# Mixing two batches' expert weights from one load, a deeper second layer for the third batch, and two-operand sums on GpSimd in an attention and feed-forward kernel

## The chip, the cores and the metric

The kernel runs on one core of one Trainium2 chip, in 32-bit floating point. The metric is the device time of one execution in microseconds (us). The kernel before the change took 3223.96 us, the median of 3 runs (3223.83 to 3225.29).

A core has five engines that run their own instruction queues in order and wait for each other by semaphores: TensorE (PE in the profile, its weight load PEld), VectorE (DVE), ScalarE (ACT), GpSimd (POOL) and SyncE (SP), which in this kernel issues all DMA transfers.

## What is computed

Four batches of 2048 tokens with 512 features go through two residual sub-layers:

```python
x = x + layernorm(attention(layernorm(x), w_qkv))   # 16 heads, windows of 128, keys of 3 windows
x = x + layernorm(ffn(layernorm(x), ...))

def ffn(x):                                   # 512 -> 2048 -> 512, 8 experts' weights mixed per batch
    g = (relu(x @ gate_w1.T + gate_b1) @ gate_w2.T + gate_b2).mean(axis=1)     # 8 numbers per batch
    mW1 = W1 + einsum('be,efh->bfh', g, TW1);  mb1 = b1 + g @ Tb1
    mW2 = W2 + einsum('be,ehf->bhf', g, TW2);  mb2 = b2 + g @ Tb2
    return gelu(x @ mW1.T + mb1) @ mW2.T + mb2
```

So each batch has weights of its own: the base plus eight experts' weights, each times one gate number. The gate numbers are means over the whole batch, so a batch's weights can be mixed only when its attention and its gate are through.

## The kernel before

**Attention stage** (the first half). It walks 256 *slots*: 64 windows of 128 tokens, four groups of four heads each. A slot puts the scores of the next slot (`scores`, L649, then the row maximum `nm`, L658, on VectorE), the transposes of this slot's probabilities (L686), some "dense" products (the projections of a later block of 512 tokens, or the gate's, L518), the exponentials (L671) and the values (L707) in a written order. What else a slot does hangs in lists by slot number: `first`, `mid`, `aux`, `rest`, `behind`, `late`; the program runs them in the order `first`, scores, transposes, `mid`, exponentials, `aux`, dense products, `rest`, the read of the second bank, weight mixing, the read of the first bank, `behind`, values, `late`.

The dense products use a Winograd form (seven half-size products for eight), which needs four sums of the transposed tokens for each block: T1 and T2 (`right_factors` part 0, L482 and L483) and T3 and T4 (part 1, L486 and L487). Both parts come once for the projections and once for the gate of a block, that is twice in 16 slots.

Each window's attention output is normalized and added to its input in `residual` (L103, L330), stored to memory, and its statistics are taken for the next normalization (`stats`: L92 and L94 on VectorE, then two one-column operations on GpSimd, L96 and L98). `normed` overwrites the same tile one slot later, so it waits for the store.

**Weight mixing** is a generator, `blend = mixer()`, that other code advances by `next(blend)`. Its order is batch, layer (`s`), chunk of 2 x 128 rows (`c`, 8 of them), expert (`e`, 8). A *step* is either one expert (one 512 KB load, issued three steps ahead into four buffers named `exps`, and one `scalar_tensor_tensor` of 128x1024 on VectorE, L155) or, after the eighth expert, the four sums that the Winograd form of the weights needs (L163 to L166, 128x256 each); the stores of a chunk are issued with the next step. In the attention, slots from 85 on take steps by the list `MIXED` (21 steps in 16 slots).

**Feed-forward stage** (the second half). It walks 16 blocks K of 512 tokens, four per batch. Each has a first layer (four sets of seven 256-wide products, L1023, in `begin`, `middle`, `end`, with the mixing steps put between products) and a second layer. For batches 0 to 2 the second layer is `second`: seven products (L1143), each 32 matmuls of 256 columns in the trace. For the last batch (`DEEP`) it is `second_deep`: Winograd applied twice, so 7 x 7 products of 128 columns (L1308), with more sums: `inner_sums` (L1233) on VectorE for the tokens' side, four GpSimd sums into `t1` at outer product `o == 2` (L1344), and `inner_mixer` (L205 to L208) for the weights' side, 14 steps that load, sum and store again what `mixer` stored. `more_sums` (L1105, L1106, L1111) and `second` (L1181, L1187) put two-operand sums on GpSimd.

Of the kernel before, what the change touches and what calls it, by code (L numbers as in the profile page):

```python
# [16 lines left out]
P = 128  # L17
# [17 lines left out]
def sandwich(ctx: ExitStack, tc: tile.TileContext, x, w_qkv, gw1, gb1, gw2, gb2, w1, b1, w2, b2, tw1, tb1, tw2, tb2, out):  # L35
# [23 lines left out]
    gw1_sb = const.tile([P, KC, D], F32, name="gw1_sb")  # L59
# [20 lines left out]
    DEEP = (NB - 1,)  # L80
# [24 lines left out]

    def mixer():

        todo = [(b, s, c, e) for b in range(NB) for s in range(2) for c in range(HC) for e in range(NX)]
        ets, accs = {}, {}
# [5 lines left out]
        def load(n):  # L115
            b, s, c, e = todo[n]
            base, exps = ((w1, tw1), (w2, tw2))[s]
            if e == 0:
                acc = mix.tile([P, 2, D], F32, tag="acc", name=f"acc_{b}_{s}_{c}")
                nc.sync.dma_start(acc, halves(base)[c])  # L120
                accs[b, s, c] = acc
            et = mix.tile([P, 2, D], F32, tag="exps", bufs=4, name=f"exps_{b}_{s}_{c}_{e}")
            nc.sync.dma_start(et, halves(exps[e])[c])
            ets[n] = et
# [20 lines left out]
        for n in range(3):  # L145
            load(n)
        yield
        for n, (b, s, c, e) in enumerate(todo):
            if n + 3 < len(todo):
                load(n + 3)  # L150
            for f in late:
                f()
            late = []
            acc = accs[b, s, c]
            nc.vector.scalar_tensor_tensor(acc, ets.pop(n), g_all[b][:, e : e + 1], acc, ALU.mult, ALU.add)  # L155
            yield
            if e == NX - 1:
                del accs[b, s, c]
# [4 lines left out]
                nc.vector.tensor_tensor(sums[:, 0, :], a21, a22, ALU.add)  # L163
                nc.vector.tensor_tensor(a21, a11, a21, ALU.subtract)
                nc.vector.tensor_tensor(sums[:, 1, :], sums[:, 0, :], a11, ALU.subtract)
                nc.vector.tensor_tensor(sums[:, 2, :], a12, sums[:, 1, :], ALU.subtract)  # L166
                late.append(lambda b=b, s=s, c=c, acc=acc, sums=sums: store(b, s, c, acc, sums))
                yield
        for f in late:
            f()  # L170

    issued = {b: 0 for b in DEEP}

    def inner_mixer(b):

        todo = [(o, h) for o in order_deep for h in range(2)]
        loaded, late = {}, []

        def load(n):
            o, h = todo[n]  # L180
            two = slice(2 * h, 2 * h + 2)
            et = mix.tile([P, 4, 2, P], F32, tag="exps", bufs=4, name=f"inner_{b}_{o}_{h}")
            nc.sync.dma_start(et[:, :2], m3_d[b][:, o, 0:8:7, two, :])
            nc.sync.dma_start(et[:, 2:], m3_d[b][:, o, 3:7:3, two, :])
            loaded[n] = et

        def store(n, et):
            o, h = todo[n]
            two = slice(2 * h, 2 * h + 2)
            nc.sync.dma_start(m3_d[b][:, o, 1, two, :], et[:, 3])  # L190
            nc.sync.dma_start(m3_d[b][:, o, 2, two, :], et[:, 0])
            nc.sync.dma_start(m3_d[b][:, o, 4:6, two, :], et[:, 1:3])
            issued[b] = n + 1

        for n in range(2):
            load(n)
        yield
        for n in range(len(todo)):
            for f in late:
                f()  # L200
            if n + 2 < len(todo):
                load(n + 2)
            et = loaded.pop(n)
            f11, f21, f12, f22 = (et[:, i] for i in range(4))
            nc.vector.tensor_tensor(f22, f21, f22, ALU.add)  # L205
            nc.vector.tensor_tensor(f21, f11, f21, ALU.subtract)
            nc.vector.tensor_tensor(f11, f22, f11, ALU.subtract)
            nc.vector.tensor_tensor(f12, f12, f11, ALU.subtract)  # L208
            late = [lambda n=n, et=et: store(n, et)]
            yield  # L210
        for f in late:
            f()

    def gate_matmuls(pm, xT, oc, kcs=range(KC)):
        for kc in kcs:
            nc.tensor.matmul(pm, lhsT=gw1_sb[:, kc, ts(oc, P)], rhs=xT[:, kc, :], start=(kc == 0), stop=(kc == KC - 1))
# [19 lines left out]
    def gate_half(pm, xT, ocs, kcs):  # L236

        for n, oc in enumerate(ocs):
            for kc in kcs[n]:
                nc.tensor.matmul(  # L240
                    pm[:, n * Q : (n + 1) * Q],
                    lhsT=gw1_sb[:, kc, ts(oc, P)],
                    rhs=xT[:, kc, :],
                    start=(n == kc == 0),
                    stop=True,
                    skip_group_check=True,
                )
# [13 lines left out]
    def gate_end(b, hsum, bank, spare):  # L261
# [24 lines left out]

        def first_biases():
# [38 lines left out]
    def residual(W_):  # L326
# [3 lines left out]
        nc.vector.tensor_tensor(x1, x1, st["x"], ALU.add)  # L330
        nc.sync.dma_start(x1_d[W_], x1)
        st["sc"] = stats(x1, f"c{W_}")
# [62 lines left out]
    with ExitStack() as actx:  # L395
# [25 lines left out]
        def load_rest():  # L421
            nc.sync.dma_start(gw1_sb, gw1.rearrange("(k p) o -> p k o", p=P))
# [36 lines left out]
        def left_factors(i):  # L459
            w = wqkv[i] if i < 3 else gw1_sb  # L460
            l11, l12, l21, l22 = (w[:, 2 * j : 2 * j + 2, h * Q : (h + 1) * Q] for h in range(2) for j in range(2))
# [12 lines left out]
        def right_factors(K, part, i=0):  # L474
# [1130 lines left out]
```

## Time and profile before

| what | value |
|---|---|
| median of 3 runs | 3223.96 us |
| the profiled execution | 3224.83 us |
| its span, first to last instruction | 3223.0 us |
| granted TensorE clock | 0.998 of full speed |
| bytes moved by DMA | 688.88 MB, mean 214 GB/s |
| mixing loads (`exps`) | 512 of 512 KB, 6.0 us to landing |

A line of "busy time" gives an engine's busy microseconds, its share of the span and its instruction count. A window line gives, for a stretch, each engine's busy time (with the number of instructions), the granted clock, the DMA engines' share and the rate. The chain of waits is followed back from the last instruction to whatever released it; its lines are start, duration and what ran. A group line gives an operation's count, its busy time and mean duration, and after the second bar the idle time before it and what ended it. A timeline line gives start, duration and the instructions.

### The profile page before, as it was taken

How to read it: one execution, taken by the hardware profiler on the slowest of the kernel's cores; microseconds unless marked ns; L12 is line 12 of the kernel's file. 1: busy time of each engine (PE TensorE's matmuls, PEld its weight loads, DVE VectorE, ACT ScalarE, POOL GpSimd, SP SyncE). 2: the span in 40 equal slices, each digit the busy share in tenths (PEclk: the TensorE clock that was granted, in tenths of full speed). 3: DMA queues.
4: the chain of work that ended last, by engine and by line, in shares of the span. 5: the costliest groups of instructions: out<-in, count | busy, mean ns of one | idle time of the engine just before them, and what ended most of it. 6: DMA issues, size and time to landing. Idle time of an engine off the chain costs nothing.

```text
span 3223.0 us, 61653 instructions
## 1 busy us (share of the span) xinstructions
PE 3197.1 (99%) x23862; PEld 2697.0 (84%) x23862; DVE 2278.8 (71%) x3307; ACT 1576.5 (49%) x4332; POOL 676.5 (21%) x847
## 2 busy tenths in 40 slices
PE   9999999999999999999999999999999999999998
PEld 7788888888788888878768888888888888889998
DVE  5766666888998889888865665677657667554555
ACT  3777777777777777777761222112222112222222
POOL 0111111111111111110112322323322323332233
PEclk9999999999999999999999999999999999999999
DMA  2111112455555556554677889999899999874555
GB/s 87 54 57 54 40 60 80 138 189 163 193 193 168 178 177 200 194 174 151 211 277 277 310 309 345 355 337 330 311 330 361 341 326 322 305 246 155 193 187 170
DMA packets 363334, 688.88 MB, mean 214 GB/s; under 512 B 27161, under 2 KB 115353, under 8 KB 357026
## 3 DMA queue, kind: packets, MB, share of 16 engines
q1 hardware_dynamic: 363042, 684.94, 61.4%
q8 instruction: 189, 3.10, 0.4%
q14 instruction: 103, 0.84, 0.1%
HBM read 567.39 MB, written 117.44 MB: 212 GB/s over the span
## 4 chain that ended last, share of the span: by engine, by line
PE 94%; DVE 2%; DMA 2%; ACT 1%; POOL 0%; issue 0%; SPq 0%; POOLq 0%; DVEq 0%; ACTq 0%
PE pm L518 23%; PE px L1023 13%; PE ptp L686 11%; PE px L1143 7%; PE sc L649 7%; PE pz L1023 6%; PE po L707 5%; PE pz L1143 5%; PE py L1023 3%; PE py L1143 3%; PE px L1308 2%; PE py2b L1143 2%; PE pz L1308 1%; PE pm L582 1%; PE ptx L340 1%; PE pto L311 1%
## 5 line engine op out<-in xcount | busy, mean ns | idle before, releaser
L155 DVE SCALAR_TENSOR_TENSOR acc<-exps,g,acc 128x1024 f32<-128x1024 f32 x512 | 697.1, 1362 | 66.1 <-DMA exps<-in_tw 60.1
L658 DVE TENSOR_REDUCE nm<-sc 128x2 f32<-128x768 f32 (+1 forms) x512 | 449.2, 918 | 206.8 <-PE sc L649 201.8
L671 ACT ACTIVATE pr<-sc,nm 128x384 f32<-128x384 f32 (+1 forms) x1024 | 572.8, 592 | 11.3 <-DVE nm L658 11.1
L691 ACT COPY prT<-ptp 128x512 f32<-128x512 f32 x732 | 382.9, 595 | 281.3 <-PE ptp L686 281.1
L686 PEld LDWEIGHTS ptp<-ident,pr 128*128 128x128 f32 x2944 | 318.0, 141 | 102.3 <-issue 89.8
L686 PE MATMUL ptp<-ident,pr 128*128 128x128 f32 x2944 | 378.7, 278 | 0.0
L1060 ACT COPY py<-px 128x512 f32<-128x512 f32 x63 | 36.0, 571 | 662.6 <-PE px L1023 662.4
L1023 PE MATMUL px<-tT,w 128*128 128x256 f32 x1512 | 350.1, 379 | 0.6 <-DVE cpv L1083 0.6
L1023 PEld LDWEIGHTS px<-tT,w 128*128 128x128 f32 x1512 | 286.9, 190 | 40.0 <-DVE cpv L1083 1.0
L649 PE MATMUL sc<-k,q 32*128 32x384 f32 (+2 forms) x2816 | 243.2, 423 | 3.7 <-ACT pr L671 3.5
L671 ACT ACTIVATION_READ_ACCUMULATOR pr<-sc,nm 128x1 f32 x1024 | 236.5, 231 | 0.0
L1080 DVE TENSOR_TENSOR cpb<-pz,cpb 128x512 f32<-128x512 f32 x63 | 43.4, 689 | 268.8 <-PE pz L1023 240.1
L96 POOL TENSOR_SCALAR ve_b<-mv_b 128x1 f32<-128x1 f32 x64 | 42.8, 669 | 819.2 <-DVE mv_b L94 819.2
L707 PEld LDWEIGHTS po<-prT,v 128*32 128x32 f32 x5888 | 152.2, 110 | 50.9 <-ACT pr L671 25.4
L707 PE MATMUL po<-prT,v 128*32 128x128 f32 x5888 | 189.7, 275 | 0.2
L649 PEld LDWEIGHTS sc<-k,q 32*128 32x128 f32 x2816 | 118.7, 184 | 74.4 <-issue 53.9
L1143 PE MATMUL px<-w2s,u 128*128 128x256 f32 x784 | 175.1, 379 | 0.0
L518 PE MATMUL pm<-xnT,wqkv 128*128 128x256 f32 x720 | 172.2, 382 | 0.0
L1105 POOL TENSOR_TENSOR t<-u 128x512 f32<-128x512 f32 x60 | 79.9, 1332 | 434.8 <-ACT u L1035 434.8
L1143 PEld LDWEIGHTS px<-w2s,u 128*128 128x128 f32 x784 | 149.0, 190 | 20.2
L518 PEld LDWEIGHTS pm<-xnT,wqkv 128*128 128x128 f32 x720 | 132.0, 190 | 16.7
L1074 ACT COPY cpb<-px 128x512 f32<-128x512 f32 x63 | 36.9, 585 | 182.0 <-PE px L1023 182.0
(295 smaller groups left out, 5911.6 us busy)
## 6 DMA issues: line engine op xcount, KB each, us to landing
exps<-in_tw SPq DMA_DIRECT2D x512, 512.0 KB, 6.0
w2s<-m2d SPq DMA_DIRECT2D x168, 512.0 KB, 8.1
w2s<-m3d SPq DMA_DIRECT2D x84, 512.0 KB, 4.7
acc<-in_w SPq DMA_DIRECT2D x64, 512.0 KB, 6.1
x<-in_x SPq DMA_DIRECT2D x64, 256.0 KB, 4.2
m1d<-acc SPq DMA_DIRECT2D x64, 256.0 KB, 6.3
w<-m1d SPq DMA_DIRECT2D x16, 1024.0 KB, 7.9
fxT<-xTd SPq DMA_DIRECT2D x16, 1024.0 KB, 8.5
```

What stands on the lines that cost most here:

```text
L155: nc.vector.scalar_tensor_tensor(acc, ets.pop(n), g_all[b][:, e : e + 1], acc, ALU.mult, ALU.add)
L518: nc.tensor.matmul(bank[u not in chain][:, half, :], lhsT=a[:, kc, ts(half, P)], rhs=b[:, kc, :], start=(u not in (2, 3, 4) and half == kc ...
L649: nc.tensor.matmul(scs[r // 2][:, r % 2, col : col + nj * W], lhsT=q[rows, g, ts(W_ % WB, W)], rhs=k_of[kb][rows, g, j0 * W : (j0 + nj) * ...
L658: nc.vector.tensor_reduce(st["nm"][:, h : h + 2], scs[u][:, :, : nk * W], AX.X, ALU.max, negate=True)
L671: nc.scalar.activation(pr[:, : nk * W], scs[r // 2][:, r % 2, : nk * W], AF.Exp, bias=st["nm"][:, h : h + 1], accum_out=st["den"][:, h : h ...
L686: nc.tensor.transpose(pt[:, r, :], st["pr"][g * 4 + r][:, ts(j, W)], ident)
L691: nc.scalar.copy(prT, pt)
L707: nc.tensor.matmul(po[r * E : (r + 1) * E, n, :], lhsT=v_of[kb][:, jj, h * E : (h + 1) * E], rhs=prT[:, r, :], start=(j == 0), stop=(j == ...
L1023: nc.tensor.matmul(bank[:, f, :], lhsT=factor[:, f, kc * P : (kc + 1) * P], rhs=right[:, kc, :], start=(start and f == 0 and kc == 0), sto ...
L1105: nc.gpsimd.tensor_tensor(t1s[c], b12, us[c][:, :, :Q], ALU.subtract)
L1143: nc.tensor.matmul(bank[:, t, :], lhsT=right(c - c % 2)[:, c % 2, ts(t, P)], rhs=w[:, c % (HC // 2), :], start=(start and c == 0 and t == ...
L1308: nc.tensor.matmul(bank, lhsT=right(p), rhs=w[:, p, :], start=(start and p == 0), stop=True, skip_group_check=True,)
```

## The change

1. **Two batches from one load.** `todo` is written out. Batches 0 and 1 stay as they are. Then come four chunks of batch 2's first layer, all eight chunks of the second layer for batches 2 and 3 together (each expert loaded once, two `scalar_tensor_tensor`), the other four chunks of the first layer for both, and batch 3's first four chunks. Batch 3's sums come two experts into the next chunk. Batch 3's accumulators lie in the gate's weight tile, which is split in two (`gw1_0`, `gw1_1`) and free once the gate is over. A step is now one `scalar_tensor_tensor`; all mixing is over in the first layer of block 8 (before: block 11).
2. **The third batch's second layer is deep too**: `DEEP = (NB - 2, NB - 1)`. Its 14 inner steps run inside `mixer`; those of the last batch run in the first layer of block 9 (before: blocks 11 and 12).
3. **Two-operand sums on GpSimd in the attention**: the residual's add, the T sums of all blocks but the first, and the mixing's four sums (33 chunks of the 64), which there no longer count as a step. The residual's store and statistics move from `rest` to `late` of the same slot.
4. **Step counts**: `MIXED` has 25 steps in 16 slots; in the feed-forward stage a block takes 39 (batch 0) or 37 (batch 1) for 34, a batch's last block 35 for 25, the first 23 for 21.
5. **Inside `second_deep`**: the four sums into `t1` go in twos to `o == 3` and `o == 4`; at `o == 6` the statistics of `y[1]` come after inner product 4 and its add, not before.

The core of the diff:

```diff
-    DEEP = (NB - 1,)
+    DEEP = (NB - 2, NB - 1)
...
+        def chunk(batches, k, c, between=()):
+            waiting = [x for x in todo if x[0] == "later"]
+            for e in range(NX):
+                todo.append(("mix", batches, k, c, e))
+                if e == 1 and waiting:
+                    todo.remove(waiting[0])
+                    todo.append(("sum", *waiting[0][1:]))
+            todo.append(("sum", batches[0], k, c))
+            for b in batches[1:]:
+                todo.append(("later", b, k, c))
+            todo.extend(("inner", *x) for x in between)
+
+        again = [(2, o, h) for o in order_deep for h in range(2)]
+        for b in range(2):
+            for k in range(2):
+                for c in range(HC):
+                    chunk((b,), k, c)
+        for c in range(4):
+            chunk((2,), 0, c)
+        for c in range(HC):
+            chunk((2, 3), 1, c)
+        for c in range(4, HC):
+            chunk((2, 3), 0, c, again[2 * c - 8 : 2 * c - 6])
+        for c in range(4):
+            chunk((3,), 0, c, again[2 * c + 8 : 2 * c + 10])
...
+            elif kind == "mix":
+                batches, s, c, e = what
+                load()
+                et = ets.pop(0)
+                for b in batches:
+                    flush()
+                    assert b in gated
+                    acc = accs[b, s, c]
+                    nc.vector.scalar_tensor_tensor(acc, et, g_all[b][:, e : e + 1], acc, ALU.mult, ALU.add)
+                    yield
...
+                engine = nc.gpsimd if attending[0] else nc.vector
+                engine.tensor_tensor(sums[:, 0, :], a21, a22, ALU.add)
+                engine.tensor_tensor(a21, a11, a21, ALU.subtract)
+                engine.tensor_tensor(sums[:, 1, :], sums[:, 0, :], a11, ALU.subtract)
+                engine.tensor_tensor(sums[:, 2, :], a12, sums[:, 1, :], ALU.subtract)
...
-    def residual(W_):
+    def residual(W_, engine=nc.gpsimd):
         st = win[W_]
         x1 = st["x1"]
         normalize(x1, st["a"], st["sb"])
-        nc.vector.tensor_tensor(x1, x1, st["x"], ALU.add)
-        nc.sync.dma_start(x1_d[W_], x1)
-        st["sc"] = stats(x1, f"c{W_}")
+        engine.tensor_tensor(x1, x1, st["x"], ALU.add)
+
+    def residual_stats(W_):
+        st = win[W_]
+        nc.sync.dma_start(x1_d[W_], st["x1"])
+        st["sc"] = stats(st["x1"], f"c{W_}")
...
-        def right_factors(K, part, i=0):
+        def right_factors(K, part, i=0, engine=nc.gpsimd):
...
-                nc.vector.tensor_tensor(t[:, 0], r12, r11, ALU.subtract)
-                nc.vector.tensor_tensor(t[:, 1], r22, t[:, 0], ALU.subtract)
+                engine.tensor_tensor(t[:, 0], r12, r11, ALU.subtract)
+                engine.tensor_tensor(t[:, 1], r22, t[:, 0], ALU.subtract)
...
+            late[i + 1].append(lambda W_=W_: residual_stats(W_))
...
-        MIXED = (1, 0, 1, 1, 2, 1, 1, 2, 2, 1, 1, 1, 2, 1, 2, 2)
+        MIXED = (2, 1, 1, 2, 2, 1, 1, 2, 2, 1, 1, 2, 2, 2, 1, 2)
...
-                if o == 2:
-                    for p in range(PAIRS2):
+                if o in (3, 4):
+                    for p in range(2 * o - 6, 2 * o - 4):
                         nc.gpsimd.tensor_tensor(t1[:, p], bottom[:, p, :, :Q], t2[p // 2][:, p % 2], ALU.subtract)
...
-                    step = mixing(0, 1, 0, 1)
+                    step = mixing(0, 1, 0, 1) if K == 0 else mixing(1, 1, 1, 1)
                 else:
-                    step = mixing(*((2, 1, 1, 1) if c == 2 else (1, 1, 1, 1)))
-                if K // NBLK in DEEP and k == 0:
+                    step = mixing(*((2, 1, 1, 1) if b == 0 or c > 2 else (1, 1, 1, 1)))
+                if K == DEEP[0] * NBLK + 1:
+                    if c == 0:
+                        assert next(blend, 0) == 0
+                        inner = inner_mixer(NB - 1)
                     step = lambda: next(inner, None)
...
-                products2 = second(K, before, mixing(3, 2, 3, 2, 2, 3, 2), load_x1)
+                products2 = second(K, before, mixing(3, 3, 3, 2, 3, 3, 2), load_x1)
```

## The prediction, made before the changed kernel ran

> **What bounds the kernel.** First the busy times, to see which engine leaves no room:
>
> ```profile
> PE 3197.1 (99%) x23862; PEld 2697.0 (84%) x23862; DVE 2278.8 (71%) x3307; ACT 1576.5 (49%) x4332; POOL 676.5 (21%) x847
> ```
>
> TensorE idles 26 us in 3223, so an edit can gain only by taking TensorE work away, and can lose by making TensorE wait. Then the windows, to see how near the other engines are to full in each stage (attention, batch 1's feed-forward, batch 3's):
>
> ```profile
> core 0: us, PE busy (x) PEld busy (x) DVE busy (x) ACT busy (x) POOL busy (x), PEclk, DMA share, GB/s
> 860.00:960.00 100.00, 100.00 (x961) 80.94 (x961) 90.10 (x132) 73.93 (x219) 13.54 (x24) 1.00 0.59 198
> ...
> 2212.00:2309.00 97.00, 97.00 (x451) 85.41 (x450) 68.56 (x78) 22.55 (x48) 29.24 (x28) 1.00 0.92 332
> ...
> 2980.00:3075.00 95.00, 93.80 (x624) 87.47 (x623) 46.94 (x99) 25.91 (x63) 29.02 (x30) 1.00 0.49 169
> ```
>
> In the attention TensorE is full and VectorE at 90%; it is the engine to overload. In batch 1 VectorE has 28 us of 97 free. The DMA is at 92%, yet TensorE is full: its transfers are hidden. Third, the chain of waits, whose second-layer entries give the length of a block:
>
> ```profile
> 2402.01 5.18 PE px L1143 x24
> ...
> 2499.21 5.18 PE px L1143 x24
> ...
> 2595.90 5.18 PE px L1143 x24
> ...
> 2693.02 5.18 PE px L1143 x24
> ...
> 2789.71 5.18 PE px L1143 x24
> ...
> 2986.57 7.45 DMA fxT<-xTd
> 3080.58 7.16 DMA fxT<-xTd
> ```
>
> Batch 2's blocks are 97.20, 96.69, 97.12 and 96.69 us apart, batch 3's deep ones 94.01. Last, how VectorE and GpSimd get on when both run two-operand operations. VectorE's timeline in block 5, and under it GpSimd's:
>
> ```profile
> 2221.35 2.25 DVE L155 SCALAR_TENSOR_TENSOR acc<-exps,g,acc 128x1024 f32<-128x1024 f32 x1
> 2223.64 1.37 DVE L163 TENSOR_TENSOR sums<-acc 128x256 f32<-128x256 f32 x1
> 2225.05 1.37 DVE L164 TENSOR_TENSOR acc<-acc 128x256 f32<-128x256 f32 x1
> ```
>
> ```profile
> 2222.58 4.96 POOL L1187 TENSOR_TENSOR u<-u,t 128x512 f32<-128x512 f32 x3
> ```
>
> A mixing operation that takes 1.278 us (L155's median) takes 2.25 here, and sums of 0.420 (L163's median) take 1.37: each waits out about 0.95 us of GpSimd's 1.27.
>
> **Part by part.** Sums are against the profiled execution, 3224.8 us (span 3223.0 and 1.8 around it); the median of the runs is 0.9 below it.
>
> *Batch 2 deep (2).* Four blocks of 387.7 us become four like batch 3's: the first 95.1 (its second layer was 1.1 us longer than the next, waiting at its start for the first inner sums), three at 94.0, together 377.1. **-10.6 us.** The inner sums' VectorE work lies where mixing was: block 8 keeps 18 steps, blocks 9 to 11 have none. Bounds: -12 (no such start) and -8 (L1308 waits twice as long).
>
> *Order in `second_deep` (5).* Batch 3 shows TensorE waiting there:
>
> ```profile
> PE px L1308 <- DVE y L1270: 5.7, 9, 1.0
> ```
>
> In TensorE's timeline these stand in each block near 19.6 us into the second layer (0.98, 0.98, 0.98 and 0.5 us), where the four `t1` sums on GpSimd push VectorE back (an inner sum of 0.68 takes 1.47 there), and at `o == 6` behind the statistics (0.55 each, 1.1 in the last). The change moves the sums to two products with two each, and the statistics back. At most -1.5 us in a block; I take -0.9 for the two new collisions, over eight blocks **-7**, bounds -12 and 0. The last block's end is VectorE's, so nothing for it there.
>
> *Sums on GpSimd in the attention (3, 4).* The T sums of the gate come 14 times from 222.7 to 1554.9 us, so 16 slots last 102.5 us. Over 660 to 1460 us VectorE is busy 89.1 of 100 us, thus 91.3 in 16 slots. Removed from it: 4 residual adds x 0.693, 8 T sums x 0.68, 2.33 chunks x 1.69 (21 steps are 2.33 x 9): 12.1. Added: 25 instead of 18.7 mixing operations x 1.278: 8.1. Leaves 87.3, **15.2 us free**. GpSimd gets 12 operations of 128x512 (1.27 us, L1105's median) and 12.5 of 128x256, which no row has: between 0.22 (L96, one column) and 1.27, I take half-way, 0.74. Together 24.5 us in 16 slots, on 13.5. What it costs VectorE by collisions: in the feed-forward stage, with GpSimd busy 29 of 97 us, the mean of L155 is 1.362 over all 512 against a median of 1.278, 43 us on some 312 operations there, 0.14 each; in the attention that makes 25 x 0.14 = 3.5 us. Here GpSimd's sums are issued just ahead of mixing operations, so I double it: 7 us, under 15.2. If every GpSimd operation met one, it would be 12 x 0.95 + 12.5 x 0.6 = 19. TensorE bears some lateness: VectorE's row maximum ends about 1 us before ScalarE uses it, and the exponentials lie ahead of the transposes by 2 us or more. T sums: near 1173 us `rs_b` ends at 1182.35, T3 on GpSimd would then be there by 1183.6, TensorE reads it at 1186.46; 2.8 us of cover, gone where four chunk sums (3 us) or a late VectorE come between. I charge **+3 us** for such stalls in 32 T3 reads, bounds 0 and +20.
>
> The Trainium skill, "SBUF — State Buffer", section "SBUF: two separate sides", speaks against this part: a VectorE operation with two SBUF inputs and a GpSimd operation lock the same port pair against each other for the whole instruction. The rows above agree in kind. Taken for every operation, with none hidden behind VectorE's reads of PSUM, it would put 24.5 us on VectorE in 16 slots and the kernel near 3307 us; by the row it is 7 us.
>
> *Store and statistics of the residual later.* The store now waits on SP behind the step's loads and chunk stores, which wait for GpSimd's sums; queued behind it are mixing loads, three steps (12 us) ahead with 6 us to landing. `normed` overwrites the stored tile one slot later: in full slots 4 us remain, but in the short last slots VectorE already waited 1.96 us for this store (at 1593.98). There GpSimd's add (1.27 for 0.69), the later issue and a step more in slots 240 and 241 add about 1 us in each of three windows: **+3 us**, bounds 0 and +8.
>
> *More steps, fewer loads (1, 4).* A block of batch 0 takes 5 more steps, 7 us of VectorE, in 28 us free: nothing on the path. In block 0, where the chain runs through VectorE from 1755 to 1782 us, two more steps of 1.28 lie half inside: **+1**, bounds 0 and 3. 96 loads of 512 KB fall away; TensorE did not wait for them: 0. If that cover were gone, VectorE's 60 us of waits for `exps` would count, and they get fewer.
>
> Sum: 3224.8 - 10.6 - 7 + 3 + 3 + 1 = 3214.2, as a median **3213 us**.
>
> **Rivals.** *A, VectorE saturates in the attention (slower).* Decides once collisions pass 15.2 us in 16 slots, 62% of GpSimd's 24.5. At the bound of 19 the excess is 3.8 us in each of (256 - 85) / 16 = 10.7 rounds: +41, so 3224.8 - 17.6 + 41 = 3248. For it: sums are issued beside mixing operations, in slots that already have two. Against: mixing holds 32 of 102 us, and the maxima and bank reads, which read PSUM, stayed at 0.69 beside GpSimd (L1080, L1163).
>
> *B, sums late on GpSimd.* T3 and T4 wait in GpSimd's queue for `ve_b`, `rs_b` (0.57 and 0.86 us near 1181) and chunk sums. At 0.5 us for each of 21 T3 reads under mixing load and the last windows at +6: 3224.8 - 17.6 + 10 + 6 + 1 = 3224, no change. For it: four queued sums use up the cover; against: they fall into one slot in five.
>
> *C, the deep blocks gain no more than TensorE's counts:* the new places of the sums collide as much (0 for -7): 3221, no change. That the change doesn't do what it says is excluded for the counts: the built program has 416 `exps` loads for 512, 56 inner loads for 28, and 831 two-operand GpSimd instructions for 516.
>
> **How the numbers follow.** Forecast 0.55 (3205 to 3219), B 0.18, C 0.09, A 0.18. About 0.2% (6.4 us) is what a measurement of this kernel can tell from no change: faster is below 3217.5, slower above 3230.4. Faster: the forecast's 0.55 less 0.03 at its upper edge, and 0.04 of B with small stalls: 0.56. Slower: A's 0.18 and 0.03 of B: 0.21. Same: 0.23. Range 3203 (both gains at their bounds, -24, with 3 of stalls) to 3236 (a third of A's excess), leaving out most of A.
>
> **What would show it.** Blocks 8 to 11 at 93 to 95 us. No L1308 wait near 19.6 us into a deep second layer. VectorE at 92 to 97% between 660 and 1460 us with L155's mean there at 1.4 to 1.6 us; 16 slots still 102.5 us long. Wrong if TensorE waits for L721 (the row maximum's new line) or L545 to L550 in full slots by more than 10 us, or if the span from slot 240 to the first layer grows by over 8 us.

## The result and the profile after

The changed kernel takes **3270.17 us** (median of 4 runs, 3269.23 to 3277.81) against 3223.89 us for the kernel before (4 runs): a ratio of 1.0149, 95% interval 1.0132 to 1.0167. It is 46 us slower; 3213 was predicted, with a range of 3203 to 3236. The profiled execution took 3270.88 us, its span is 3269.1.

The busy times of the changed kernel:

```profile
PE 3204.8 (98%) x24534; PEld 2714.3 (83%) x24534; DVE 2275.9 (70%) x3309; ACT 1591.7 (49%) x4376; POOL 1067.4 (33%) x1162
```

VectorE's busy time is that of before to 3 us, GpSimd's grew from 676 to 1067. Over the whole span no engine ran out; the time is in waits, and the stages have to be compared. Block lengths below run from one block's last second-layer matmul to the next one's, in the profiled execution of each:

| stretch | before, us | after, us | difference |
|---|---|---|---|
| attention and block 0's first layer | 1711.1 | 1737.2 | +26.1 |
| blocks 0 to 5 | 544.2 | 543.2 | -1.0 |
| blocks 6, 7, 8, 9 | 96.7, 96.7, 97.2, 96.7 | 98.9, 108.3, 103.7, 106.0 | +29.6 |
| blocks 10, 11 | 97.1, 96.7 | 93.4, 93.4 | -7.0 |
| blocks 12 to 15 | 95.1, 94.0, 94.0, 94.2 | 94.4, 93.4, 93.4, 92.9 | -3.2 |
| behind the last matmul | 9.4 | 10.9 | +1.6 |

The deep second layer does what was forecast (blocks 10 and 11). Two stretches lose far more, and both losses begin with a transfer that an engine working in order stands and waits for. The windows show where to look: the same attention stretch as before, then block 7 and a block of batch 3:

```profile
860.00:960.00 100.00, 98.14 (x917) 78.78 (x916) 86.75 (x114) 70.18 (x209) 40.42 (x46) 0.98 0.65 217
2379.00:2487.00 108.00, 100.19 (x448) 86.75 (x447) 65.38 (x88) 22.37 (x48) 29.64 (x27) 0.97 0.99 363
2980.00:3075.00 95.00, 94.19 (x626) 87.92 (x625) 46.59 (x99) 25.55 (x60) 29.52 (x33) 1.00 0.50 176
```

In the attention GpSimd went from 13.5 to 40.4 us of 100, TensorE from 100 to 98.1 with a clock of 0.98, and VectorE from 90 *down* to 87: it was not too full, it stood still. In block 7 the DMA engines are at 0.99 and VectorE at 65 of 108.

**The attention.** What VectorE, then TensorE waited for between 560 and 1640 us after the change:

```profile
DVE x L103 <- DMA x1d<-x: 24.5, 12, 4.4
```

```profile
PE sc L712 <- ACT pr L734: 10.0, 21, 1.6
```

The columns are total, times and longest. Before, the first line read 6.6 us in 2 waits and the second 1.6 in 6. L103 is `normed`, and `x1d<-x` the residual's store: it overwrites the tile and must wait until the store has read it. One such place, in the order in which it arises; first GpSimd's timeline:

```profile
858.02 1.27 POOL L389 TENSOR_TENSOR x<-x,xr 128x512 f32<-128x512 f32 x1 [0.36 <-DVE x L103]
859.25 0.73 POOL L262 TENSOR_TENSOR sums<-acc 128x256 f32<-128x256 f32 x1
860.06 1.73 POOL L263 TENSOR_TENSOR acc<-acc 128x256 f32<-128x256 f32 x1
861.74 0.73 POOL L264 TENSOR_TENSOR sums<-sums,acc 128x256 f32<-128x256 f32 x1
862.55 0.72 POOL L265 TENSOR_TENSOR sums<-acc,sums 128x256 f32<-128x256 f32 x1
```

SP's, which issues the stores:

```profile
862.50 0.34 SPq L213 DMA_DIRECT2D m1d<-sums  x1
863.30 0.85 SPq L214 DMA_DIRECT2D m1d<-sums  x1
864.19 0.44 SPq L215 DMA_DIRECT2D m1d<-acc  x1
864.67 0.45 SPq L393 DMA_DIRECT2D x1d<-x  x1
```

And VectorE's:

```profile
867.30 0.55 DVE L103 TENSOR_SCALAR x<-x,mv_c,rs_c 128x512 f32<-128x512 f32 x1 [2.51 <-DMA x1d<-x]
867.77 0.68 DVE L855 TENSOR_TENSOR g<-pm,g 128x512 f32<-128x512 f32 x1
868.37 3.99 DVE L251 SCALAR_TENSOR_TENSOR acc<-exps,g,acc 128x1024 f32<-128x1024 f32 x2
872.28 1.27 DVE L721 TENSOR_REDUCE nm<-sc 128x2 f32<-128x512 f32 x2
```

The add is through at 859.3, and the tile could go then. But its store stands in `late`, on SP behind the chunk's stores, and these wait for GpSimd's sums: the store is issued 5.4 us after its data were there. `normed` waits 2.51 us for it; behind it in VectorE's queue stand two mixing operations (3.99 us, one of them next to T sums on GpSimd) and the row maximum, which ends at 873.5; ScalarE's exponentials wait for that and TensorE for them, 1.64 us.

**Blocks 6 to 9.** VectorE's line for the mixing loads between 2280 and 2700 us, and TensorE's two lines for what comes of it between 2050 and 2600 us:

```profile
DVE acc L251 <- DMA exps<-in_tw: 42.3, 22, 5.0
```

```profile
PE px L1088 <- DVE cpv L1148: 6.3, 2, 5.6
PE py L1088 <- ACT py L1125: 6.2, 2, 4.4
```

Before, the longest wait for `exps` in these blocks was 3.7 us, and TensorE's waits for VectorE and ScalarE between 2050 and 2600 us came to 0.2 us. Now a wait of 5 us holds up VectorE's reads of PSUM behind it, and TensorE has no bank to write. The place in block 7, VectorE's last inner sum and what follows it, then TensorE:

```profile
2419.44 0.42 DVE L120 TENSOR_TENSOR inner<-inner 128x256 f32<-128x256 f32 x1
...
2427.42 1.28 DVE L251 SCALAR_TENSOR_TENSOR acc<-exps,g,acc 128x1024 f32<-128x1024 f32 x1 [5.02 <-DMA exps<-in_tw]
...
2432.59 0.68 DVE L1148 TENSOR_TENSOR cpv<-px,cpv 128x512 f32<-128x512 f32 x1
```

```profile
2433.32 3.78 PE L1088 MATMUL px<-tT,w 128*128 128x256 f32 x8 [5.60 <-DVE cpv L1148]
```

From about the start of block 7 the mixing is batch 3's last four chunks (32 mixing operations in blocks 7 and 8): each expert's step needs a load of its own again, and between them stand batch 2's inner steps, two at a time. Each of these holds one of the four `exps` buffers until its stores are through.

Block 9's loss is one wait; its first layer holds all 14 inner steps of the last batch, and VectorE waits 12.0 us in four times for their loads. TensorE between 2590 and 2700 us:

```profile
PE px L1088 <- DVE cpv L1148: 9.5, 1, 9.5
```

**The deep blocks' own wait** near 20 us into the second layer is still there. VectorE, then TensorE in block 10, whose second layer begins at 2743.8:

```profile
2757.82 1.46 DVE L1298 TENSOR_TENSOR inner_right<-u,inner_right 128x512 f32<-128x512 f32 x1
2759.87 1.09 DVE L427 TENSOR_TENSOR tT<-fxT 128x512 f32<-128x512 f32 x1 [0.59 <-DMA fxT<-xTd]
2760.88 0.28 DVE L1335 TENSOR_TENSOR y<-pz,y 128x128 f32<-128x128 f32 x1
...
2762.76 1.56 DVE L1298 TENSOR_TENSOR inner_right<-u,inner_right 128x512 f32<-128x512 f32 x1
2764.24 0.28 DVE L1335 TENSOR_TENSOR y<-px,y 128x128 f32<-128x128 f32 x1
```

```profile
2764.57 1.16 PE L1373 MATMUL px<-w2s,inner_right 128*128 128x128 f32 x8 [0.82 <-DVE y L1335]
```

VectorE stands at the first sum for the *next* block, `tT`, until that block's tokens have landed, and the inner sums around it take 1.3 to 1.6 us for 0.68; the reads of PSUM (L1335) come behind both.

### The profile page after: what moved, and what is told of

The parts are those of the page before. It is cut to its first block, busy times and chain, and to the rows that moved or that the text cites. A ratio compares the mean times of both kernels' runs of the same rounds, so it can differ in the third digit from the quotient of the medians.

```text
span 3269.1 us, 63660 instructions
## 1 busy us (share of the span) xinstructions
PE 3204.8 (98%) x24534; PEld 2714.3 (83%) x24534; DVE 2275.9 (70%) x3309; ACT 1591.7 (49%) x4376; POOL 1067.4 (33%) x1162
## 4 chain that ended last, share of the span: by engine, by line
PE 83%; DMA 7%; DVE 6%; issue 2%; POOL 2%; ACT 1%; SPq 1%; DVEq 0%; POOLq 0%; ACTq 0%
PE pm L581 20%; PE px L1088 12%; PE ptp L749 10%; PE sc L712 6%; PE pz L1088 6%; PE po L770 5%; PE px L1373 5%; PE px L1208 4%; PE pz L1208 3%; PE py L1088 3%; DMA exps<-in_tw 3%; PE pz L1373 2%; DMA fxT<-xTd 2%; DVE acc L251 1%; PE py L1208 1%
## 5 line engine op out<-in xcount | busy, mean ns | idle before, releaser
L251 DVE SCALAR_TENSOR_TENSOR acc<-exps,g,acc 128x1024 f32<-128x1024 f32 x512 | 717.5, 1416 | 50.2 <-DMA exps<-in_tw 46.0
L712 PE MATMUL sc<-k,q 32*128 32x384 f32 (+2 forms) x2816 | 251.4, 422 | 12.7 <-ACT pr L734 12.4
L96 POOL TENSOR_SCALAR ve_b<-mv_b 128x1 f32<-128x1 f32 x64 | 50.9, 795 | 553.3 <-DVE mv_b L94 553.3
L712 PEld LDWEIGHTS sc<-k,q 32*128 32x128 f32 x2816 | 122.5, 183 | 89.0 <-issue 51.6
L1373 PE MATMUL px<-w2s,inner_right 128*128 128x128 f32 x1344 | 178.9, 276 | 7.7 <-DVE y L1335 7.7
L1373 PEld LDWEIGHTS px<-w2s,inner_right 128*128 128x128 f32 x1344 | 163.9, 192 | 9.6 <-DVE y L1335 9.6
L1400 ACT COPY py<-px 128x128 f32<-128x128 f32 x56 | 14.0, 250 | 271.4 <-PE px L1373 182.9
```

Of the source, the lines that this page charges most:

```text
L251: nc.vector.scalar_tensor_tensor(acc, et, g_all[b][:, e : e + 1], acc, ALU.mult, ALU.add)
L712: nc.tensor.matmul(scs[r // 2][:, r % 2, col : col + nj * W], lhsT=q[rows, g, ts(W_ % WB, W)], rhs=k_of[kb][rows, g, j0 * W : (j0 + nj) * ...
L1373: nc.tensor.matmul(bank, lhsT=right(p), rhs=w[:, p, :], start=(start and p == 0), stop=True, skip_group_check=True,)
```

## The experiments

All times are medians, beside runs of the kernel before on the same chip (3223.5 to 3224.8 us). "Product" is the start of block 0's second layer in the profiled execution: 1711.1 before, 1737.2 after. It is one reading per run: four runs below (experiments 3, 4, 5 and 7) leave the attention stage as changed and read 1732.7 to 1734.8, so the attention's loss is 22 to 26 us, and a difference of up to some 4 us between two such readings shows nothing by itself.

**1. The residual's store.** It is issued right behind the add, the statistics stay in `late`:

```diff
         engine.tensor_tensor(x1, x1, st["x"], ALU.add)
+        nc.sync.dma_start(x1_d[W_], x1)
...
-        nc.sync.dma_start(x1_d[W_], st["x1"])
```

> The changed kernel with the store of the residual issued directly behind its add in the list rest, ahead of the slot's mixing loads and chunk stores on SP; the add stays on GpSimd, the statistics stay in late. Theory Q (queue): of the 26 us that the attention lost (first second-layer product at 1737.2 us for 1711.1), most come from VectorE waiting in normed for a store that SP holds behind chunk stores, which wait for GpSimd's sums; then the start comes back to 1718 to 1724 us and the time falls to 3250 to 3257 us. Rival L (locks): VectorE is late because GpSimd's two-operand sums lock it out; all those sums are still there, so the start stays at 1732 us or later and the time at 3264 us or more.

Measured: 3254.98 us, ratio 1.0097 (1.0082 to 1.0112), product 1720.3. VectorE's waits for this store fell from 24.5 to

```profile
DVE x L103 <- DMA x1d<-x: 8.0, 4, 2.9
```

So one line's place on SP is 15 us of the total. By the products it is 12 to 17 of the 22 to 26 us that the attention lost, as theory Q says.

**2. The chunk sums back on VectorE**, everything else as changed (`engine = nc.vector` for the four sums).

> The changed kernel with only the four chunk sums of the mixing back on VectorE in the attention (not counted as a step); residual adds and T sums stay on GpSimd. Theory Q: the chunk stores no longer wait for GpSimd's queue, so the waits of normed for the store nearly vanish; VectorE gets 3.1 x 1.7 = 5 us more in 16 slots and stays below full: start of the first second layer at 1715 to 1726 us, time 3247 to 3259 us. Rival L: 9 of 24.5 us of GpSimd's locks go but VectorE's own work grows by 5 us, so little changes: start 1730 us or later, time 3262 us or more.

Measured: 3286.1 us, 1.0189 (1.0173 to 1.0204), product 1752. The store's waits went to 7.0 us as the queue theory says, but VectorE now has these sums too, and TensorE's line L712 grew to 13.2 us. Theory Q's numbers are missed. Rival L's bounds are met, but it expected little change, and this kernel is 16 us slower than the changed one. VectorE's work grew from 700 to 734 us between 660 and 1460 us; why that costs more here than 764 us do in experiment 6 was not found. Taking a wait away with work on the same engine tests two things at once.

**3. The last batch's inner steps**, 5, 5 and 4 in the first layers of blocks 9, 10 and 11, at every second place, instead of all 14 in block 9.

> The changed kernel with the last batch's 14 inner steps spread: five, five and four in the first layers of blocks 9, 10 and 11, at every second place, instead of all in block 9 at every place. Theory D (transfers): block 9 lost 12 us (106.0 for 93.4) because VectorE stood in its queue behind inner sums whose loads had not landed; with twice the distance the loads land in time and block 9 takes 93 to 95 us, blocks 10 and 11 stay at 93.4, time 3257 to 3260 us. Rival V (VectorE's own work): the 24 us of inner sums themselves push back the reads of PSUM; then the loss is only spread, blocks 9 to 11 take about 97 us each and the time stays above 3266 us.

Measured: 3258.3 us, 1.0108 (1.0091 to 1.0125); block 9 takes 93.4 us. Confirmed.

**4. Steps earlier**: 42 steps in each of blocks 1 to 6 but block 3, which takes 38 (42: second layer 4, 3, 3, 3, 3, 3, 3; first layer 2, 1, 1, 1).

> The changed kernel with more steps in blocks 1 to 6 (42 in a block and 38 in block 3, for 39, 37 and 35), so that block 7 has some 20 left instead of 35 and block 8 none. Theory D: blocks 7 and 8 lost 20 us together (108.3 and 103.7 us) because single-batch loads, the next batch's weights and inner loads and stores meet there with the DMA at 0.99; with steps moved to blocks whose DMA share is 0.78 they take 198 us or less together (212 before), blocks 1 to 6 stay at 96.7 to 98, time 3252 to 3262 us. Rival V: VectorE's steps are what pushes back its reads of PSUM; then blocks 1 to 6 get longer by 2 us or more each and the time is 3270 us or above.

Measured: 3273.48 us, 1.0155 (1.0140 to 1.0170); block 5 takes 98.2, block 7 120.6, block 8 94.8. Theory D is missed, and rival V's total is met without its sign, since blocks 1 to 4 take what they took in the changed kernel. Block 7 held fewer steps (19 mixing operations and 4 inner steps for 23 and 6) and lost more: 13 and 4 of them stood in its first layer, for 9 and 4, and TensorE waited 10.2 and 8.8 us in this block. So the number of steps in a block does not set its loss by itself; how closely they follow each other may, and experiment 7 tries that.

**5. The next block's sums one product later.**

```diff
-                if o == 2 and not last_block:
+                if o == 3 and not last_block:
...
-                if o in (2, 3, 6):
+                if o in (3, 4, 6):
```

> Edit: in the deep second layer the sums for the next block's first layer (tT, L427) begin at outer product 3 instead of 2. Question: what makes TensorE wait 0.98 us near 19.6 us into every deep second layer, which moving the t1 sums did not end. Theory F (VectorE stands at the first of these sums until the next block's tokens, fxT, have landed, 7.4 us after their issue, and the bank reads behind it come late): the wait goes or shrinks below 0.3 us, in 7 deep blocks with a successor -0.7 to -1 us each: 3263 to 3266. Rival G (it comes from GpSimd's t1 sums or from the inner sums themselves): the wait stays, 3269 to 3272.

Measured: 3267.26 us, 1.0133 (1.0118 to 1.0148); deep blocks at 92.9 for 93.4. Between 2600 and 3250 us TensorE's waits for VectorE in the deep second layer, first after the change and then here:

```profile
PE px L1373 <- DVE y L1335: 6.1, 8, 0.8
```

```profile
PE px L1373 <- DVE y L1335: 3.0, 7, 0.8
```

The wait in block 10 fell from 0.82 to 0.37 us, not below the 0.3 of theory F: the wait for the load was the cause of about half of it. By the total alone the intervals overlap, and the block lengths carry the verdict.

**6. All three moves to GpSimd undone** (residual with store and statistics together, T sums, chunk sums on VectorE), with the 25 steps and the feed-forward stage as changed.

> Edit: all three moves to GpSimd in the attention undone (residual's add, store and statistics together on VectorE as before; T sums and the chunk sums on VectorE), but the 25 mixing steps in 16 slots and everything in the feed-forward stage kept. It shows what the moves buy. By counts VectorE would have 91.3 + 8.1 + 1.4 = 100.8 us of work in 102.5 us of 16 slots. Theory V (that is too full; in-order waits lengthen the slots): first second-layer product of block 0 at 1745 to 1790 instead of 1737, total 3278 to 3325. Rival N (the moves buy nothing, their waits on SP and in GpSimd's queue cost more than they save): first product at 1712 to 1725, total 3245 to 3258.

Measured: 3265.01 us, 1.0126 (1.0111 to 1.0141), product 1731.2. Neither theory's numbers are met. VectorE is nearly full as theory V says, 764 us of 800 between 660 and 1460, and the attention loses 20 us, for 22 to 26 with the moves. As they were made, the moves gained nothing; that they cost something is not shown, since the intervals of the totals overlap (1.0132 to 1.0167 for the changed kernel).

**7. The single steps slower**: 39 steps in blocks 4 to 6, 25 in block 7, the rest in block 8's first layer.

> Edit: the last 44 steps (batch 3's single chunks and batch 2's inner steps) are put at a lower rate: blocks 4 to 6 take 39 steps for 37, block 7 takes 25 for 35, block 8's first layer the rest (up to 20). Theory P (blocks 7 and 8 are long because each of these steps needs a transfer of its own through four buffers, and 35 in a block ask more than the transfers give; before the change 34 such steps stood in a block and 25 in a batch's last): block 7 takes 97 to 101 us for 108.3 and block 8 95 to 99 for 103.7, total 3253 to 3261. Rival W (the work of these blocks is too much for VectorE or the DMA in whatever order; moving steps moves the loss): blocks 4 to 8 together stay within 5 us of after's 504.3, total 3265 to 3275.

Measured: 3252.56 us, 1.0091 (1.0076 to 1.0106); blocks 6 to 8 at 96.7, 100.2 and 96.9 for 98.9, 108.3 and 103.7. Confirmed, with 3.5 us left in block 7.

**8. Edits 1, 3 and 7 together.**

> Edit: three of the edits together: the residual's store directly behind its add, the last batch's inner steps in thirds over the first layers of blocks 9 to 11, and the slower single steps. If the three losses are separate, their gains add: store 15.3, thirds 12, singles 10 to 16 from 3270: 3227 to 3233, still no faster than the kernel before, because the attention keeps 9 us of its 26. If they share a cause (the DMA), the sum comes out above 3240.

Measured: 3223.9 us, 0.9999 (0.9989 to 1.0008): the gains of the three add (15.2, 11.9 and 17.6 us, together 44.7; measured 46.3), so the losses are separate. The kernel is back at the time of before.

**9. Four variants of edits 1, 3, 5 and 7**, with a still lower rate for the single steps (34 in block 6, 18 in block 7): as they are, with 22 attention steps for 25, with the residual on VectorE, with the T sums on VectorE.

> Edit: the residual's store directly behind its add, the inner steps in thirds, the next block's sums from outer product 3, and the single steps at a still lower rate (42, 42, 42, 39, 39, 34, 18 and up to 15 steps in blocks 1 to 8). Theory S (the losses are separate and their gains add): the four-edit run without the third edit gave 3223.9; -0.45 in 7 deep blocks is -3, block 7 from 101.5 to 97 or 98 is -4: 3215 to 3219. Rival (block 7's last loss comes from the batch's own loads, not the rate): block 7 stays at 100 to 102 us, 3219 to 3222.

> Edit: as the four edits, and 22 mixing steps in 16 attention slots for 25; blocks 1 to 5 take 45 steps, block 6 39. Theory V (the 8 to 9 us which the attention still loses with the store put first come from VectorE's mixing work): 30 fewer steps give most of it back, first second-layer product at 1711 to 1715 for 1719.5, and blocks 1 to 5 stay at 96.7 since VectorE has 28 us free there: 3208 to 3214. Rival G (they come from waits on GpSimd's queue, T sums and residual): first product stays at 1717 to 1720; 3215 to 3220.

> Edit: as the four edits, but the residual's add, store and statistics stand together on VectorE as in the kernel before, instead of an add on GpSimd with the store behind it; T sums and chunk sums stay on GpSimd. Theory V (VectorE's load sets the remaining loss): 2.8 us more work in 16 slots, first product 1719 to 1726, 3217 to 3226. Rival G (the residual's wait in GpSimd's queue sets it): first product 1712 to 1716, 3209 to 3214.

> Edit: as the four edits, but the T sums of all blocks on VectorE; residual's add (store behind it) and chunk sums stay on GpSimd. Theory V (VectorE's load): 5.4 us more in 16 slots, first product 1721 to 1730, 3219 to 3230. Rival B of the prediction (T3 comes late on GpSimd): first product 1711 to 1716, 3208 to 3214.

| | us | ratio (interval) | product | blocks 5 to 8 |
|---|---|---|---|---|
| four edits | 3224.58 | 1.0001 (0.9992 to 1.0011) | 1718.5 | 98.0, 99.1, 103.7, 94.4 |
| 22 steps | 3254.74 | 1.0100 (1.0085 to 1.0115) | 1713.4 | 101.2, 104.0, 101.0, 104.6 |
| residual on VectorE | 3224.88 | 1.0002 (0.9993 to 1.0012) | 1716.7 | 98.6, 99.7, 102.2, 94.3 |
| T sums on VectorE | 3222.14 | 0.9994 (0.9984 to 1.0003) | 1716.6 | 98.3, 98.3, 101.2, 94.3 |

The totals of the first two miss what was expected; those of the last two lie in theory V's ranges, but the later product that it rests on (1719 or more) did not come. A lower rate did not help block 7 further, so rate was not its whole cause. With 22 steps the product came 5 us earlier, as theory V says, but the 45 steps which blocks 1 to 5 then took did not fit: block 2 alone took 105.9 us. And either move undone is worth some 2 us by the profile, which is no more than two readings of the product can differ, and nothing by the totals. What block 7 still waits for stands in VectorE's timeline of the first variant:

```profile
2363.85 0.42 DVE L117 TENSOR_TENSOR inner<-inner 128x256 f32<-128x256 f32 x1
...
2366.93 0.42 DVE L120 TENSOR_TENSOR inner<-inner 128x256 f32<-128x256 f32 x1
...
2369.60 1.28 DVE L251 SCALAR_TENSOR_TENSOR acc<-exps,g,acc 128x1024 f32<-128x1024 f32 x1
2373.85 1.28 DVE L251 SCALAR_TENSOR_TENSOR acc<-exps,g,acc 128x1024 f32<-128x1024 f32 x1 [2.98 <-DMA exps<-in_tw]
...
2383.40 1.28 DVE L251 SCALAR_TENSOR_TENSOR acc<-exps,g,acc 128x1024 f32<-128x1024 f32 x1 [3.63 <-DMA exps<-in_tw]
```

Two inner steps in direct succession are 3.4 us of VectorE and two of the four buffers, given back only after their stores; the loads behind them come late. That the buffers are the reason is a reading of these lines, tested next.

**10. The inner steps among the pairs**: batch 2's 14 inner steps singly between the experts of the four pair chunks, where one load serves two steps; edits 1, 3, 5 and 7 besides.

```diff
+                if e in between and e < NX - 1:
+                    todo.append(("inner", *again.pop(0)))
...
-            chunk((2, 3), 0, c, again[2 * c - 8 : 2 * c - 6])
+            chunk((2, 3), 0, c, ((4, 6, 7), (1, 3, 5, 7), (1, 3, 5, 7), (1, 4, 7))[c - 4])
```

> Edit: store first, last batch's inner steps in thirds, next block's sums from outer product 3, single steps at 39, 39, 39, 25 in blocks 4 to 7; and batch 2's 14 inner steps no longer stand in twos behind each of eight chunks, four of these single ones, but singly between the experts of the four pair chunks, where a load serves two steps. Theory B (two inner steps in succession take two of the four load buffers, and the loads behind them come late): block 7 falls from 101.5 to 97 to 98 us and block 8 to 95 to 96; blocks 4 to 6 stay at 96.7 to 97.5; total 3212 to 3218. Rival (block 7's own transfers, deep weights among them, are too many): block 7 stays above 100, 3219 to 3224.

Measured: 3219.35 us, 0.9985 (0.9976 to 0.9994); blocks 5 to 8 at 99.1, 96.7, 96.7 and 96.6. Block 7's loss is gone, as theory B says; block 5 has a new one of 2.4 us, and the total lies just above B's range. The edit takes the inner steps apart and also out of the single steps of blocks 7 and 8; which of the two was needed is not shown.

**11. Besides that, T sums and residual on VectorE**, alone and with 24 attention steps for 25.

> Edit: as the run with the inner steps among the pairs, but residual (with store and statistics together) and T sums on VectorE as in the kernel before; only the chunk sums stay on GpSimd, with 25 steps in 16 slots. Theory G (waits in GpSimd's queue are what the attention still loses): first second-layer product at 1711 to 1715, and against the run beside it -4 to -7 us. Rival V (VectorE's load, 8.2 us more in 16 slots, costs as much as the waits did): first product 1717 to 1725, 0 to +6 against the run beside it.

> Edit: as the run with T sums and residual on VectorE, and 24 steps in 16 slots for 25; blocks 1 to 3 take 42. Theory G: VectorE's load does not matter, first product within 1 us of the run beside it. Rival V: 1 to 3 us earlier; blocks 1 to 3 stay at 96.7 by either.

Measured: 3217.09 us, 0.9978 (0.9969 to 0.9988), product 1715.0 for 1719.1; and 3220.07 us, 0.9987 (0.9978 to 0.9996), product 1716.8 (block 1 took 102.3). The product leans to theory G, but the same attention stage reads 1716.6 in experiment 12, between the two theories; by the totals the gain of 2 us is within the intervals, and less than G's 4 to 7. One step fewer gains nothing.

**12. Batch 3's sums four experts behind batch 2's**, not two (`if e == 3 and waiting` for `e == 1`), on the first kernel of 11.

> Edit: as the run with T sums and residual on VectorE, and batch 3's sums come four experts into the next chunk, not two. If block 5's loss comes from the single sums buffer, block 5 is 96.7 to 97 us for 98.9 and the total 3213 to 3216; if not, block 5 stays above 98 and the total at 3216 to 3219.

Measured: **3215.28 us, 0.9974 (0.9964 to 0.9984)**, the lowest median of all; blocks 5 to 7 at 96.7, block 8 at 95.2, blocks 9 to 11 at 93.0. Block 5's loss is gone, as expected if it came from the single sums buffer. In block 7 the DMA engines are almost as busy as in the changed kernel's (0.97 for 0.99), and TensorE loses nothing:

```profile
2360.00:2456.00 96.00, 96.00 (x447) 84.57 (x446) 53.74 (x66) 22.43 (x48) 29.84 (x28) 1.00 0.97 354
```

## Why the prediction was wrong, point by point

- *Batch 2 deep, -10.6*: right in mechanism and size. Blocks 10 and 11 of the changed kernel gained 7.0, and in the last experiment blocks 8 to 11 take 374.1 us for 387.7, of which some 0.5 a block is experiment 5's and some 0.6 the change inside `second_deep` (batch 3's blocks: 94.0 to 93.4). The sentence on where the inner sums' work would lie was wrong: block 8 holds 9 mixing operations, two inner steps and two chunks' sums, not 18 steps, and block 9 all 14 inner steps of the last batch.
- *Store and statistics of the residual later, +3*: **the step that failed first**. It said that "in full slots 4 us remain" and charged only the short last slots. It had itself named the chain (chunk stores wait for GpSimd's sums, the store stands behind them), but put no time on that wait. In the example the store went out 5.4 us after its data; VectorE waited twelve times between 560 and 1640 us, 24.5 us in all, most of them in full slots, and the place cost 15 us (experiment 1). Of before it read one wait for this store, 1.96 us; a second one, at 1620.87 us, took 4.60.
- *More steps, fewer loads, nothing on the path*: **the second failure, and the larger one**, +29.6 us in blocks 6 to 9, for which the sum has nothing (its +1 is for block 0). It reasoned from totals: 96 loads fewer, 28 us of VectorE free, `exps` waits "get fewer". But the loads that went were the pairs'; what was left for blocks 7 and 8 were 32 single mixing operations with their sums and eight inner steps among them, in four shared buffers, and the last batch's 14 inner steps all in one first layer (block 9). Before, the inner steps stood in blocks 11 and 12, seven in each, beside at most 8 mixing operations. Experiments 3, 7 and 10 took this loss away without changing how much is loaded; that the four buffers are the reason fits all of them, but was not tested by itself.
- *Order in `second_deep`, -7*: half right. Before, TensorE waited for VectorE 0.4 us (1.0 in the last block) near 47 us into the second layer of each deep block, at `o == 6`; these waits are gone. The wait near 20 us was put down to the `t1` sums, and it stayed when they moved: a wrong cause. Half of it is a load, and that stood in the chain shown from before: `fxT<-xTd`, in the deep blocks. Blocks 12 to 15 gained 3.2 and the end gave back 1.6 (probably because VectorE's statistics of `y[1]` come later there), so about 1 to 2 us for batch 3.
- *GpSimd's collisions, 7 us in 16 slots, hidden*: the size was nearer to the row than to its doubling. Between 560 and 1575 us L251's mean is 1.397 us, with a longest of 2.31; L155's was 1.277 with a longest of 1.29. That is 25 x 0.12 = 3.0 us. The sign "L155's mean there at 1.4 to 1.6 us" (L251 now) was just missed, at 1.396 between 660 and 1460 us; "VectorE at 92 to 97%" was missed too (87.5; 89.4 with the store first), as the collisions cost less than the 7 us that it counted with. A high share is no loss in itself: in the last experiment, with T sums and residual on VectorE, it is 93.5%. What was left out is GpSimd's side of the collisions (last section), though a row of the prediction had it: three GpSimd operations of 1.27 us took 4.96.
- *Rival A* (VectorE saturates, 3248) had the right sign for the wrong reason: VectorE was 87.5% busy. In experiment 6, with VectorE at 95%, the attention loses 20 us. *Rival B* (GpSimd's queue late, 3224) was nearer: T sums and residual together are 2 to 5 us of product (1718.5 to 1720.3 in four readings with them on GpSimd and the store first, 1715.0 and 1716.6 without). But not by the reads it named: TensorE has no wait for a T sum in the changed kernel, so the +3 us that the sum charges for 32 T3 reads was not seen either. Neither rival named SP.
- *Open*: with only the chunk sums on GpSimd the product still comes 4 to 5.5 us later than before. Fewer steps moved it in one experiment (5 us, 22 steps) and not in another (24 steps); it was not settled whether VectorE's load or the rest of the waits is behind it.

## What to carry to other kernels

A step that is moved has to be followed on every queue that it issues on: an operation put on another engine takes the DMA issues that wait for it along, and everything behind them on an in-order queue. Free time of an engine and a lower total of loads say little about a stretch; count buffers, loads and steps there, block by block, and ask what the first late load holds up. When a change loses, mend its placements one at a time before giving up its idea: here the change with five placements mended and two of its three moves to GpSimd taken back beats the kernel before by 0.26%.

## What the runs showed of the hardware

**A wait costs more than its length.** TensorE in the changed kernel's block 8:

```profile
2505.86 3.78 PE L1088 MATMUL py<-fxT,w 128*128 128x256 f32 x8 [4.39 <-ACT py L1125]
2509.44 4.46 PE L1088 MATMUL px<-tT,w 128*128 128x256 f32 x16
...
2515.46 1.89 PE L1088 MATMUL px<-tT,w 128*128 128x256 f32 x8
```

Eight matmuls that take 1.89 us take 3.78 behind the wait: the second starts 0.588 us after the first and the next 11 every 0.427 us instead of 0.216, which adds 2.7 us to a wait of 4.4. The granted clock of the stretch shows it, in block 7 behind the wait of 5.6 us:

```profile
2433.00:2441.00 8.00, 7.68 (x22) 6.25 (x23) 1.55 (x2) 1.75 (x4) 1.26 (x1) 0.60 1.01 397
```

PE is "busy" 7.68 of 8 us at 0.60 of its clock, so a wait hides in the busy share and shows in the clock. The Trainium skill, "TensorE: Matmul & The Clock Gate", Part 1, "What's actually happening", says that TensorE falls to half its clock after an idle window of about 3.4 us and comes back after a busy window of the same length. The waits of 4.4 and 5.6 us agree with the fall; from their ends TensorE worked 5.3 and 6.1 us at the slow pace, longer than one such window. Shorter waits did it too: in the attention example above TensorE was busy for 3.2 of the 5 us from 871 to 876, and the window from 876 to 880 us has a clock of 0.57.

**GpSimd suffers from collisions as much as VectorE.** Between 560 and 1575 us a chunk sum of 128x256 takes 0.73 us alone (the half-way estimate was 0.74) and 0.92 to 1.08 on average, some 32 us over its 116 operations; VectorE's 233 mixing operations lose 28 us. The second T sum takes 1.86 us for 1.27, and a one-column operation that takes 0.22 us alone takes 1.16 beside a mixing operation. That happened before too, 17 times in 40, and 35 times in 39 after the change; the averages, before and after:

```profile
L96 POOL TENSOR_SCALAR ve_b<-mv_b 128x1 f32<-128x1 f32 x40 | 32.0, 799 | 500.5 <-DVE mv_b L94 500.5
```

```profile
L96 POOL TENSOR_SCALAR ve_b<-mv_b 128x1 f32<-128x1 f32 x39 | 41.6, 1066 | 293.6 <-DVE mv_b L94 293.6
```

The T sums on GpSimd brought it there: with them back on VectorE the average is 0.80 again (first part of experiment 11, and the last variant of 9), with the residual alone back it stays at 1.07.

The Trainium skill, "SBUF — State Buffer", section "SBUF: two separate sides", describes a lock that either side can hold, so this agrees with it; the prediction applied it to VectorE alone.
